# Cross-attention and slot experts on one core: which queue loads the context of batches 4 to 15

## The chip, the core and the metric

The kernel runs on one core of a Trainium2 chip. A core has a matrix engine (TensorE, in profiles PE, with its weight loads as PEld), a vector engine (VectorE, DVE), a scalar engine with activation tables (ScalarE, ACT), a general engine (GpSimd, POOL) and SyncE (SP), which here does nothing but issue DMAs. Each works through its own instructions in order and waits on semaphores for the others. DMAs can be issued by SP, ACT or POOL; all run on the core's 16 DMA engines.

The metric is the time of one execution on the device in microseconds (us), the median of several runs. Before the change it is 1179.04 us over 3 runs (1178.51 to 1179.66).

## What is computed

16 batches of 100 tokens with 256 features attend to a context of 361 rows each, with 16 heads of 16 features; then a layer of 16 soft experts with 64 slots each follows. All is float32.

```python
x = x + xattn(layernorm(x), ctx, ctx, mask, wq, bq, wk, bk, wv, bv, wo, bo)
x = x + ffn(layernorm(x), ...)

# xattn: q = query @ wq + bq; k = ctx @ wk + bk; v = ctx @ wv + bv; 16 heads
#        softmax(q k^T / 4 + (1 - mask) * -1e9) @ v @ wo + bo
# ffn:   x = layernorm(x) * g + b; se = layernorm(slot_embeds) * scale
#        logits = x . se                                   # 100 tokens x 1024 slots
#        dispatch = softmax over tokens; combine = softmax over slots
#        slots = dispatch^T x
#        eout = (gelu(slots Wg + bg) * (slots Wu + bu)) Wd + bd     # 16 experts
#        out = combine @ eout
```

## The kernel before

**Groups and streams.** The batches go in groups of 2, 2, 4, 4 and 4 (`GROUPS`). For each group the attention of its batches runs first, then the softmaxes over tokens and slots, then the 16 experts on the slots of all its batches. Expert weights (512 KB a piece) are streamed from memory once per group through six buffers (`w_all`, `load_weights`, L1209, issued by SP). While the experts of one group run, the attention of the next is worked in between their matmuls.

**The order is a plan.** The program keeps a model of the engines (`Clock`): every piece of work adds an assumed duration to its engine's time. Each piece is a Python generator wrapped in a `Task`; before it goes on, it yields the time from which it may run. The main loop picks the task that is ready, and TensorE's order, and with it that of every other engine, is the order in which tasks are stepped. So an assumed duration or due time changes no computation, but changes the order of instructions. Before the first expert matmul the loop also emits `warm_up` matmuls (L1329), which compute nothing that is used, where it expects TensorE to be idle. Real waits are made by semaphores, whatever the plan assumed.

**Context and keys.** `load_kv(b)` loads the context of batch b into `c_sb`, of which there are two buffers. For b < 4 the rows come as they are, in two DMAs (L199, L202), and TensorE transposes them (L584). For b >= 4 the context comes in 32 x 32 blocks, so that VectorE's block transpose can turn it (L594, L595): twelve DMAs, for each of four blocks of partitions two of 32 partitions x 11 x 32 elements (L210, 352 pieces of 128 bytes, 44 KB) and one of 32 x 2 x 32 (L213, 64 pieces, 8 KB). `load_kv(b + 1)` is called at the start of `key_work(b)`, which makes keys (`k_ps`, L609) and values (`v_ps`, L669) of batch b. `kv_t[b]` is the time from which the plan lets the transposes of batch b run.

**Attention.** For each batch and each of four blocks of four heads: scores for the row maximum (`maxima`, L781, reduced at L786), the maximum folded into the queries (`queries`, L795 and L797), scores again and exponentials (`exponentials`, L806, L814), product with the values (`values`, L829). `out_work(b)` divides by the sums: a shuffle and a reciprocal on VectorE (L709, L710), a product `cxs` on GpSimd (L713), and for every second block the sum of two (L717, VectorE). Then come the output projection `o_ps` (L722), a normalisation (statistics L436, L437; `rstd` on VectorE, L444, then a power on GpSimd, L447), `xn` (L743, VectorE), its transpose `xn_t` (L748) and `xnT` (L754, ScalarE).

**Dispatch and experts.** `lg` (L938) are the logits; the softmax over tokens has its maximum on VectorE (L963), exponentials on ScalarE (L968), and the product `d_ex` by the reciprocal sums on VectorE for group 0 and GpSimd for later ones (L993). `d_t` (L1016) turns it with TensorE (groups 0 to 2), L1008 with VectorE (groups 3 and 4); `sl` (L1028) are the slots. Expert matmuls are `gp` and `up` (L1275) and `dn` (L1235), with the activation on ScalarE (L1286) and the product on VectorE (L1291); `po` (L1157) combines.

**GpSimd's queue before.** In the first 15 us it clears tiles and issues eight DMAs (parameters at L264 to L267, the slot embeddings at L400). From then on it has only the small products named above, and issues nothing.

The lines that the change is about:

Of the kernel before, what the change touches and what calls it, by code (L numbers as in the profile page):

```python
# [43 lines left out]
SB = 352  # L44
# [85 lines left out]
def xattn_ffn_kernel(  # L130
# [27 lines left out]
    nc = tc.nc  # L158
    ctx.enter_context(tc.manual_schedule())
    ck = Clock(4)  # L160
# [17 lines left out]
    def load_x(g):  # L178

        accs[g] = two.tile([N, NG, D], F32, tag="acc", name="acc", bufs=3)  # L180
        step = 2 if g else 1
        for i in range(0, GROUPS[g], step):
            b = starts[g] + i
            nc.sync.dma_start(
                accs[g][:, i : i + step, :], x[b : b + step].rearrange("b n d -> n b d")
            )
            if b == 0:
                load_kv(0)
        x_t[g] = ck.t["PE"] + 7.0 if g else 3.9

    loads, kv_t = {}, {}

    def load_kv(b):

        c_sb = two.tile([P, 3, D], F32, tag="c_sb", name="c_sb")
        if b < 4:
            nc.sync.dma_start(  # L199
                c_sb[:KC, 0:2, :], kv[b, : 2 * KC].rearrange("(c p) d -> p c d", p=KC)  # L200
            )
            nc.sync.dma_start(c_sb[: S2 - 2 * KC, 2, :], kv[b, 2 * KC :])  # L202
        else:
            c_sb = c_sb.rearrange("p c d -> p (c d)").rearrange("p (k s) -> p k s", k=KD)
            blocks = kv[b, :SB].rearrange("(b y) (k a x) -> a y k b x", y=32, a=4, x=32)
            last = kv[b, S2 - 32 :].rearrange("y (k a x) -> a y k x", a=4, x=32)
            for a in range(4):
                rows = c_sb[32 * a : 32 * a + 32]
                for kd in range(KD):
                    nc.sync.dma_start(  # L210
                        rows[:, kd, :SB].rearrange("y (b x) -> y b x", x=32), blocks[a, :, kd]
                    )
                nc.sync.dma_start(rows[:, :, SB:], last[a])  # L213
        loads[b] = c_sb
        kv_t[b] = ck.t["PE"] + 6.0 if b else 5.4

    w_sb = {}

# [113 lines left out]
    def late_loads():  # L332

        nc.vector.tensor_scalar(mrow, mrow, -1.0, 1e9, ALU.add, ALU.mult)
        ck.run("DVE", 0.35)
        nc.sync.dma_start(mrow_d, mrow)
        load_kv(1)
        nc.sync.dma_start(wo_sb, wo.rearrange("(k p) o -> p k o", p=P))
        nc.sync.dma_start(bo_bc, bo.partition_broadcast(P))
# [230 lines left out]
    def key_work(b):  # L570
# [3 lines left out]
        if b + 1 < B and b + 1 not in loads:  # L574
            load_kv(b + 1)
# [942 lines left out]
```

## Time and profile before

| | us |
|---|---|
| median of 3 runs | 1179.04 |
| the profiled execution | 1181.03 |
| its span, first to last instruction | 1179.2 |
| first use of a block-wise context: L594 of batch 4 | 194.9 |
| first issue of L210, by SP | 55.4 |
| last issue of L213, by SP | 658.9 |
| SP's issues of L210, 96, median | 0.464 |
| SP's issues of L213, 48, median | 0.574 |
| POOL's own DMA issues, 8, shortest and longest | 0.52 and 0.96 |

The span is what the trace covers; the execution's own time has some 1.8 us more around it. Times in the profile are counted from the span's start. An engine's busy share is the union of its instructions' times. "Idle before" in a timeline line, in square brackets, is how long the engine had nothing to do before the instruction, with what ended that wait. SP's and ACT's issues of DMAs don't count as busy; on POOL a DMA shows as an instruction that holds the engine. A float32 matmul shows as two passes, so that counts of passes in the trace are twice those of the code for most matmuls.

### The profile page before, as it was taken

The page shows a single profiled execution, that of the slowest core. Times are in us where ns is not written, and L with a number is a line of the kernel's source. Part 1 is how long each engine was busy: PE and PEld are TensorE (multiplying, and loading weights), DVE is VectorE, ACT ScalarE, POOL GpSimd, SP SyncE. Part 2 cuts the span into 40 slices and gives each one's busy share as a digit, 9 for nine tenths or more (in the row PEclk, how much of TensorE's full clock was granted, in tenths as well). Part 3 has the DMA queues.
Part 4 walks back from the last instruction along what each step waited for, and adds up shares of the span by engine and source line. Part 5 has one row for each costly group of instructions (what it writes and reads, how often), then busy time and mean ns, then how long its engine had stood idle before and what let it go on. Part 6 is the DMA issues. An engine that isn't in the chain of part 4 may idle for free.

```text
span 1179.2 us, 24287 instructions
## 1 busy us (share of the span) xinstructions
PE 1160.4 (98%) x9815; PEld 898.6 (76%) x9815; DVE 633.4 (54%) x1559; ACT 540.3 (46%) x1112; POOL 151.4 (13%) x255
## 2 busy tenths in 40 slices
PE   8899999999999999999999999999999999999998
PEld 6588788787788877767777776787878878777876
DVE  5755445566654566655386767656543455432222
ACT  3547553565544667434454634646312336314110
POOL 3110301013000131300010010304000003002000
PEclk9999999999999999999999999999999999999999
DMA  4412666553466603223341321333344343344441
GB/s 133 133 33 83 233 195 202 163 140 120 130 221 224 188 11 90 83 53 106 112 106 54 110 90 39 98 126 112 112 159 138 115 148 126 112 132 159 140 129 55
DMA packets 138578, 144.85 MB, mean 123 GB/s; under 512 B 45040, under 2 KB 97218, under 8 KB 138466
## 3 DMA queue, kind: packets, MB, share of 16 engines
q1 hardware_dynamic: 137358, 141.60, 39.7%
q8 instruction: 78, 1.28, 0.4%
q0 software_dynamic: 496, 1.12, 0.3%
q10 hardware_dynamic: 612, 0.57, 0.2%
q14 instruction: 34, 0.28, 0.1%
HBM read 141.60 MB, written 1.66 MB: 121 GB/s over the span
## 4 chain that ended last, share of the span: by engine, by line
PE 95%; DVE 2%; ACT 2%; issue 1%; DMA 0%; POOL 0%; SPq 0%; ACTq 0%; DVEq 0%; POOLq 0%
PE dn L1235 19%; PE gp L1275 19%; PE up L1275 19%; PE sl L1028 5%; PE po L1157 5%; PE at L806 4%; PE at L781 4%; PE lg L938 3%; PE cx L829 3%; PE k_ps L609 3%; PE v_ps L669 3%; PE o_ps L722 1%; PE at L1329 1%; DVE mxp L786 1%; PE q_ps L538 1%; ACT d_ex L968 1%
## 5 line engine op out<-in xcount | busy, mean ns | idle before, releaser
L1275 PE MATMUL gp<-ring,w_all 128*128 128x256 f32 (+1 forms) x1280 | 247.8, 340 | 1.3 <-ACT lg_all L959 1.3
L1275 PE MATMUL up<-ring,w_all 128*128 128x256 f32 (+1 forms) x1280 | 246.6, 340 | 0.0
L1291 DVE SCALAR_TENSOR_TENSOR hT<-up,parT,ge 128x256 f32<-128x256 f32 (+1 forms) x320 | 119.7, 424 | 233.2 <-PE up L1275 164.3
L1235 PE MATMUL dn<-w_all,hT 128*64 128x256 f32 x2048 | 232.9, 382 | 0.1
L1286 ACT ACTIVATE ge<-gp,parT 128x256 f32<-128x256 f32 (+1 forms) x320 | 117.1, 430 | 249.3 <-PE gp L1275 245.2
L1275 PEld LDWEIGHTS gp<-ring,w_all 128*128 128x128 f32 x1280 | 203.4, 191 | 27.5 <-issue 4.9
L1275 PEld LDWEIGHTS up<-ring,w_all 128*128 128x128 f32 x1280 | 203.7, 191 | 21.4 <-issue 1.2
L1235 PEld LDWEIGHTS dn<-w_all,hT 128*64 128x64 f32 x2048 | 142.7, 137 | 78.5 <-issue 7.8
L786 DVE TENSOR_REDUCE mxp<-at 100x4 f32<-100x1444 f32 x64 | 106.3, 1661 | 30.9 <-PE at L781 30.2
L1244 DVE TENSOR_TENSOR ring<-dn,bd_bc 128x512 f32<-128x512 f32 x64 | 44.3, 692 | 134.8 <-PE dn L1235 133.2
L814 ACT ACTIVATE aT<-at 121x1200 f32<-121x1200 f32 x64 | 75.0, 1171 | 62.9 <-PE at L806 59.5
L1286 ACT ACT_TABLE_LOAD x60 | 77.0, 1283 | 26.7 <-PE gp L1275 26.0
L1008 DVE STREAM_TRANSPOSE disp<-d_ex 32x128 f32<-32x128 f32 x256 | 77.3, 302 | 4.5
L713 POOL TENSOR_TENSOR cxs<-cxs,rs 128x100 f32<-128x100 f32 x63 | 24.9, 398 | 389.3 <-DVE rs L710 361.9
L1043 ACT ACTIVATE ring<-sl,parT 128x256 f32<-128x256 f32 x64 | 32.7, 562 | 67.8 <-PE sl L1028 65.5
L1028 PE MATMUL sl<-disp,xn 100*128 100x256 f32 x256 | 63.4, 388 | 0.2 <-ACT disp L1021 0.2
L1157 PE MATMUL po<-ring,lg_all 128*100 128x256 f32 x256 | 60.5, 383 | 0.4 <-DVE ring L1244 0.2
L993 POOL TENSOR_TENSOR d_ex<-d_ex,d_sm 128x400 f32<-128x400 f32 x28 | 23.9, 854 | 267.6 <-DVE d_sm L990 240.6
L806 PEld LDWEIGHTS at<-q,kT 32*121 32x121 f32 x1344 | 40.6, 180 | 19.9 <-issue 8.8
L1028 PEld LDWEIGHTS sl<-disp,xn 100*128 100x128 f32 x256 | 46.4, 190 | 10.3 <-issue 2.6
L806 PE MATMUL at<-q,kT 32*121 32x100 f32 x1344 | 49.9, 277 | 3.4 <-DVE q L797 3.3
L814 ACT ACT_TABLE_LOAD x36 | 46.2, 1283 | 14.2 <-PE at L806 6.2
(152 smaller groups left out, 1268.8 us busy)
## 6 DMA issues: line engine op xcount, KB each, us to landing
w_all<-in_L_ffn_Wg_dram SPq DMA_DIRECT2D x80, 512.0 KB
w_all<-in_L_ffn_Wu_dram SPq DMA_DIRECT2D x80, 512.0 KB
w_all<-in_L_ffn_Wd_dram SPq DMA_DIRECT2D x80, 512.0 KB
bd_bc<-in_L_ffn_bd_dram SPq DMA_DIRECT2D x80, 64.0 KB
c_sb<-in_ctx_dram SPq DMA_DIRECT2D x96, 44.0 KB
out_dram<-acc SPq DMA_DIRECT2D x8, 200.0 KB
acc<-in_x_dram SPq DMA_DIRECT2D x7, 200.0 KB
ring<-n_L_ffn_slot_embeds_dram POOLq DMA_DIRECT2D x1, 1024.0 KB, 6.8
```

Of the source, the lines that this page charges most:

```text
L781: nc.tensor.matmul(self.at[:N, r, :S2], lhsT=self.q[rows], rhs=self.k[rows], start=True, stop=True)
L786: nc.vector.tensor_reduce(mxv[:, :, m : m + 1], self.at[:N, :, :S2], AX.X, ALU.max, negate=True)
L806: nc.tensor.matmul(self.at[: KC + 1, r, c * N : (c + 1) * N], lhsT=self.k[rows, c * KC : c * KC + KC + 1], rhs=self.q2[rows], start=True, ...
L814: nc.scalar.activation(self.aT[: KC + 1], self.at[: KC + 1, :, : 3 * N], AF.Exp)
L1008: nc.vector.transpose(dst[toks, :, :, a, :], src[32 * a : 32 * a + 32, :, :, toks])
L1028: nc.tensor.matmul(sl[:, kd * 256 : (kd + 1) * 256], lhsT=xns[g][:, b0 + i, kd * P : (kd + 1) * P], rhs=disp[:, i, :], start=True, stop=True,)
L1157: nc.tensor.matmul(pos[i][:N, :D], lhsT=lg_all[:, slot, 2 * c + i, :], rhs=eouts_of(g, q)[:, c, 2 * p + i, :], start=c == 0, stop=c == 1,)
L1235: nc.tensor.matmul(dn[S * x : S * x + S, i * D : (i + 1) * D], lhsT=hts[x][fc // FB][0].rearrange("p (f b s) -> p f b s", f=FB, s=S)[:, fc ...
L1244: nc.vector.tensor_tensor(eouts_of(g, q)[:, j // 2, 2 * half : 2 * half + 2, :], dn.rearrange("p (b d) -> p b d", d=D), biases[k // 2].uns ...
L1275: nc.tensor.matmul(ps[:, f * T : (f + 1) * T], lhsT=w[:, kd, fc * P : (fc + 1) * P], rhs=slots_of(g, q)[:, j, kd].rearrange("p b s -> p (b ...
L1286: nc.scalar.activation(ge[:, cols], ps[:, cols], AF.Gelu, bias=col(8, e, fc))
L1291: nc.vector.scalar_tensor_tensor(out=hT[:, cols], in0=ps[:, cols], scalar=col(NPAR, e, fc), in1=ge[:, cols], op0=ALU.add, op1=ALU.mult,)
```

## The change

The twelve loads of batches 4 to 15 are issued on GpSimd's queue. The plan is told: 12 x 0.6 us are added to GpSimd's time at each of these loads, and their transposes may run 14 us of planned TensorE time after the call, instead of 6.

```diff
             for a in range(4):
                 rows = c_sb[32 * a : 32 * a + 32]
                 for kd in range(KD):
-                    nc.sync.dma_start(
+                    nc.gpsimd.dma_start(
                         rows[:, kd, :SB].rearrange("y (b x) -> y b x", x=32), blocks[a, :, kd]
                     )
-                nc.sync.dma_start(rows[:, :, SB:], last[a])
+                nc.gpsimd.dma_start(rows[:, :, SB:], last[a])
         loads[b] = c_sb
-        kv_t[b] = ck.t["PE"] + 6.0 if b else 5.4
+        if b >= 4:
+            ck.run("POOL", 12 * 0.6)
+        kv_t[b] = ck.t["PE"] + (14.0 if b >= 4 else 6.0) if b else 5.4
```

Because the plan's times differ, the order of instructions differs on every engine from batch 4's load on. The counts are the same but for 144 DMA issues that move from SP to POOL, 6 more of the `warm_up` matmuls (54 for 48), 6 more activation table loads on ScalarE (126 for 120), and one copy of values (L680) that is on VectorE where it was on ScalarE (L683). On GpSimd, the first load's twelve issues stand between two `cxs` products (L713) of batch 1:

```
TensorTensor cxs<-cxs,rs 128x100
DMACopy c_sb<-in_ctx_dram 32x11x32 x2
DMACopy c_sb<-in_ctx_dram 32x2x32
...
TensorTensor cxs<-cxs,rs 128x100
TensorTensor rstd<-rstd,neghalf 100x1
```

## What was predicted

> **What bounds the kernel now.** I read the page's busy line and its chain of work first, then windows by stage, then the waits of PE, then the timeline around the place where the change first acts. Line numbers are those of the kernel before; the changed kernel's are two higher from L217 on.
>
> ```profile
> PE 1160.4 (98%) x9815; PEld 898.6 (76%) x9815; DVE 633.4 (54%) x1559; ACT 540.3 (46%) x1112; POOL 151.4 (13%) x255
> PE 95%; DVE 2%; ACT 2%; issue 1%; DMA 0%; POOL 0%; SPq 0%; ACTq 0%; DVEq 0%; POOLq 0%
> ...
> 0.00:90.00 90.00, 80.52 (x787) 61.28 (x788) 54.21 (x144) 43.43 (x92) 20.59 (x57) 0.98 0.35 101
> 90.00:390.00 300.00, 298.42 (x3186) 239.28 (x3186) 163.47 (x400) 163.98 (x333) 35.59 (x58) 1.00 0.55 173
> 390.00:450.00 60.00, 57.66 (x417) 44.88 (x415) 36.74 (x90) 40.05 (x116) 17.82 (x24) 1.00 0.27 71
> ```
>
> TensorE is busy 98% of the span and is 95% of the chain. The windows (length, then busy time of PE, PEld, DVE, ACT, POOL, then granted clock, DMA share, GB/s) show where the 18.8 us without PE work lie: 9.5 before 90 us, 1.6 in the next 300, 2.3 around 390 to 450 (the same view has 1.0 between 600 and 630 and 4.3 after the last matmuls). The clock is 1.00 after the start, so it takes no part. Two things follow. A transfer that comes sooner can win next to nothing: no DMA ends a wait of PE among PE's waits. And the start is a bare chain: what is late there comes off no slack, because from about 84 us (the first expert matmul) PE has as much work as it can do until the end.
>
> **What leaves SyncE.** 144 issues, 96 of L210 at a median 0.464 us and 48 of L213 at 0.574, together 96 x 0.464 + 48 x 0.574 = 72 us of SP's time. Gain: 0. SP's own waits say why.
>
> ```profile
> SPq L1209 <- PE dn L1235: 349.7, 34, 26.2
> SPq L1209 <- PE gp L1275: 222.3, 42, 13.8
> ```
>
> Issuing the expert weights (L1209), SP waits for TensorE to give weight buffers back; it isn't short of time. Had PE been waiting for weights, up to the 2.3 us of the window 390 to 450 could come back; I take nothing. What stood behind these issues on SP comes sooner, by up to the 6.9 us that the first load took (55.4 to 62.3): the x rows of L184 at 62.3, first read at 73.8, so that wins nothing. The bytes and their 36,864 pieces of 128 B (12 loads of 8 x 352 + 4 x 64) are the same.
>
> **What arrives on GpSimd.** Twelve loads of 12 issues. How long one holds the engine is not in the trace for 352 pieces of 128 B. The rows nearest to it:
>
> ```profile
> 5.76 0.74 POOL L264 DMA_DIRECT2D ring<-in_L_ffn_slot_g_dram  x1
> ...
> 7.05 0.52 POOL L264 DMA_DIRECT2D ring<-in_L_ffn_norm_g_dram  x1
> ...
> 8.67 0.57 POOL L266 DMA_DIRECT2D ring<-in_L_ffn_bu_dram  x1
> 9.21 0.60 POOL L267 DMA_DIRECT2D sc_bc<-in_L_ffn_scale_dram  x1
> ...
> 11.76 0.96 POOL L400 DMA_DIRECT2D ring<-n_L_ffn_slot_embeds_dram  x1
> ```
>
> Second column: us held. Two pieces take 0.52 to 0.74, 64 take 0.57, 128 take 0.60, 1024 take 0.96, and each starts when the one ahead ends: issues on POOL are serial. Between 0.56 and 0.96, 352 pieces stand at 0.56 + 0.40 x 352/1024 = 0.70, and L213's 64 at 0.56. A load is then 8 x 0.70 + 4 x 0.56 = 7.8 us of POOL. Bounds: 12 x 0.52 = 6.2 and 8 x 0.96 + 4 x 0.74 = 10.6. In all some 94 us (75 to 128) on an engine that is 13% busy; as a sum this costs nothing, as a block in an in-order queue it does.
>
> The changed order gives the POOL issues eight completion semaphores in turn, so the ninth issue waits for the first to land. POOL's landings in the trace took 2.0 to 4.7 us, and 6.8 for 1 MB; eight issues take 6 x 0.70 + 2 x 0.56 = 5.3. I take 0 for it, and 6.8 - 5.3 = 1.5 per load at the far end.
>
> POOL's other work shows no disturbance: L713 took 395/397/403 ns (minimum, median, maximum) over 63 executions, with VectorE busy 54% around it. [...]
>
> **Where the first block stands.** load_kv(4) is called when batch 3's keys begin. SP ran ahead and issued it at 55.4. In POOL's new order the 12 issues stand behind the cxs product (L713) of 65.17 and ahead of the next one.
>
> ```profile
> 65.17 0.40 POOL L713 TENSOR_TENSOR cxs<-cxs,rs 128x100 f32<-128x100 f32 x1 [0.53 <-DVE rs L710]
> ...
> 67.39 0.40 POOL L713 TENSOR_TENSOR cxs<-cxs,rs 128x100 f32<-128x100 f32 x1 [1.82 <-DVE rs L710]
> ...
> 69.03 0.25 DVE L717 TENSOR_TENSOR cxs<-cxs 128x100 f32<-128x100 f32 x1
> ...
> 69.53 1.03 PE L722 MATMUL o_ps<-wo_sb,cxs 128*100 128x256 f32 x4
> ...
> 73.92 0.39 PE L748 MATMUL xn_t<-ident,xn 100*128 100x100 f32 x2
> ...
> 75.03 1.18 PE L938 MATMUL lg<-xnT,seT 128*128 128x200 f32 x6
> ```
>
> Step A: the block runs from 65.57 to 65.57 + 7.8 = 73.4; the product to 73.8; the sum L717 to 74.1; the output projection o_ps starts at about 74.3 where it was 69.53: 4.8 us late. Nothing covers it: k_ps and v_ps stand behind o_ps on PE, and the matmuls just ahead of it (L1329) are filler that computes nothing. Also behind the product on POOL are both rstd (L447), which the same chain needs later. At the bounds A is 3.2 and 7.6.
>
> Step B: the new order also puts the last two v_ps matmuls and 6 more fillers ahead of lg, and on DVE two copies of v_ps ahead of xn. From o_ps: 0.86 + 0.45 filler + 1.22 + 1.73 + 0.45 + 0.88 (their parts of the chain of waits) = 5.6, then copy 0.42, xn 0.40 and two hand-overs, xn_t at about 6.7, lg 1.1 later: 7.8. Before, o_ps to lg took 75.03 - 69.53 = 5.5. B = 2.3; at the least 1.0, if the copy doesn't hold xn.
>
> **The other eleven blocks** meet a PE that has expert work, except where a group of batches changes. There the ninth batch's neighbours matter: the new POOL order is rstd, 12 issues, then two d_ex products (L993) that the transposes d_t (L1016) await. PE has between them k_ps 2.8, o_ps 1.0, x_t 0.5, v_ps 2.9, q_ps 1.5 = 8.7 us; the block and one product are 7.8 + 0.85 = 8.7. So 0, and at 10.6 a stall of 2.8; a second such spot follows within the same group: another 2.8. The loads are needed late: the changed plan allows 14 us from call to use, against 7.8 + 4.7 = 12.5. Six more table loads on ACT (126 for 120) at 1283 ns are 7.7 us on an engine idle 54%; were that cover gone they would cost these 7.7.
>
> **Sum.** 4.8 + 2.3 + 0 = 7.1 us on a profiled execution of 1181.03 (span 1179.2 and 1.8 around it): 1188.1. That execution was 2.0 above the median 1179.04, so the median becomes 1186.1. Low end: 3.2 + 1.0 = 4.2, 1183. High end: 7.6 + 2.3 + 2.8 + 2.8 = 15.5, or with 1.5 of landing at three spots instead 11.6: 1194.5.
>
> **Rivals.** *The issue is dearer than any row* (256 more pieces than L267, short ones, eight in a row). At 1.2 and 0.8 a block is 12.8: A 9.8, B 2.3, two stalls of 12.8 + 0.85 - 8.7 = 5.0 each: 22 us, 1201. For it: the price does grow with the pieces. Against: 1024 pieces took 0.96. *Not slower:* the engine is free again long before its issue is done. The product of 67.39 has slack to L717 at 69.03, so A is zero if twelve issues fit in 69.03 - 0.40 - 65.57 = 3.1 us, 0.26 each; then the new order, with 1.6 + 2.3 + 1.0 = 4.9 us of idle PE between 90 and 630 us to win back, ends at 1174 to 1180. Against: the serial rows above, and a MEMSET that follows L400 only after its 0.96. *The load lands after its use*, in the changed plan's 14 us: the transposes (L594) then hold VectorE's queue; if weight traffic delayed the last landing to 16, 2 us at each of twelve loads, 24, and A and B: 31 in all, 1210. Against: SP's first load, among the same traffic, was issued from 55.4 to 62.3 us, and no L594 waited more than 1.1 us for its data. That the loads don't move at all is excluded by the order.
>
> **How the numbers follow.** Forecast 0.58 (1183 to 1194), dearer issue 0.22, late landing 0.07, not slower 0.13. 0.2% is 2.4 us, about what a measurement here tells from no change. Faster by more needs the rival below 1176.7: 0.03; within it the rest of that case: 0.10; slower 0.87. The range takes the forecast, two thirds of the dearer case and the upper edge of no change: 1181.5 to 1199.
>
> **What would show it.** Right: 12 POOL issues behind a cxs of about 65 us, held 0.6 to 0.8 each; o_ps at 74 and the first gp about 7 us later than before; PE busy time the same; later stalls only at d_t. Wrong: issues under 0.3 us or over 1; o_ps on time; a wait of PE for a DMA; L594 waiting for c_sb; or a start as told and an end that gives it back.

## The result, and the profile after

The changed kernel takes 1189.37 us (median of 4 executions, 1188.26 to 1190.71) where the kernel before takes 1179.22 (4 executions, 1178.51 to 1179.66): a ratio of 1.0082, 95% interval 1.0069 to 1.0096. Two further sets of executions gave 1.0070 (1.0056 to 1.0085) and 1.0073 (1.0059 to 1.0086). The profiled execution took 1188.49, with a span of 1186.6: 7.4 more than the span before. Lines from L217 on stand two higher than in the kernel before: `cxs` is L715, its sum L719, `o_ps` L724, `lg` L940, `gp` L1277.

The page's busy line and chain:

```profile
PE 1164.3 (98%) x9827; PEld 901.6 (76%) x9827; DVE 635.3 (54%) x1560; ACT 547.1 (46%) x1117; POOL 239.3 (20%) x399
PE 93%; ACT 3%; DVE 1%; DMA 1%; POOL 1%; issue 1%; SPq 0%; DVEq 0%; ACTq 0%
```

The windows (length, then busy time of PE, PEld, DVE, ACT, POOL, then granted clock, DMA share, GB/s):

```profile
0.00:90.00 90.00, 77.12 (x752) 56.78 (x753) 52.08 (x140) 37.49 (x76) 27.95 (x69) 0.96 0.33 95
90.00:390.00 300.00, 298.24 (x3163) 240.58 (x3163) 164.79 (x402) 162.69 (x337) 64.96 (x106) 1.00 0.53 169
390.00:450.00 60.00, 57.59 (x521) 44.01 (x518) 36.89 (x88) 36.12 (x102) 27.48 (x42) 1.00 0.31 98
```

POOL is busy for 88 us more, the 144 issues. After 90 us TensorE's busy share is what it was (298.24 for 298.42, 57.59 for 57.66), so most of the time is lost ahead of that. There its idle time grew only from 9.5 to 12.9 us; the rest must be time in which TensorE was busy, but slower or with other work. The clock of that window, 0.96 for 0.98, points to the first of these.

The timeline of POOL and of PE around the first block (start, duration, and in brackets the idle time before with what ended it):

```profile
64.22 0.40 POOL L715 TENSOR_TENSOR cxs<-cxs,rs 128x100 f32<-128x100 f32 x1 [0.53 <-DVE rs L712]
65.25 1.36 POOL L210 DMA_DIRECT2D c_sb<-in_ctx_dram  x2 [0.64 <-PE c_t L586]
66.61 0.56 POOL L213 DMA_DIRECT2D c_sb<-in_ctx_dram  x1
...
70.84 1.29 POOL L210 DMA_DIRECT2D c_sb<-in_ctx_dram  x2
72.12 0.56 POOL L213 DMA_DIRECT2D c_sb<-in_ctx_dram  x1
72.70 0.41 POOL L715 TENSOR_TENSOR cxs<-cxs,rs 128x100 f32<-128x100 f32 x1
```

```profile
67.25 1.50 PE L1331 MATMUL at<-ident 128*128 128x128 f32 x12
68.58 0.59 PE L724 MATMUL o_ps<-wo_sb,cxs 128*100 128x256 f32 x2
73.46 0.91 PE L724 MATMUL o_ps<-wo_sb,cxs 128*100 128x256 f32 x2 [4.28 <-DVE cxs L719]
74.16 1.06 PE L1331 MATMUL at<-ident 128*128 128x128 f32 x4
75.02 2.45 PE L611 MATMUL k_ps<-cT,wk 128*128 128x361 f32 x4
...
81.43 1.52 PE L940 MATMUL lg<-xnT,seT 128*128 128x200 f32 x8
...
90.52 1.72 PE L1277 MATMUL gp<-ring,w_all 128*128 128x128 f32 x14
```

The block waits 0.64 us for its buffer, issues for 7.43 us, and the product behind it comes at 72.70 where it came at 67.39. The second half of `o_ps` waits 4.28 us for it. Behind that wait the same matmuls take longer than they did: four fillers 1.06 us for 0.61, `k_ps` 2.45 for 1.38. The windows of that stretch have the granted clock in the same column as above:

```profile
72.00:74.00 2.00, 0.54 (x2) 0.49 (x3) 0.26 (x1) 0.00 (x0) 1.09 (x3) 0.94 0.20 49
74.00:75.00 1.00, 1.00 (x5) 0.91 (x5) 0.56 (x2) 0.00 (x0) 0.00 (x0) 0.50 0.00 0
75.00:76.00 1.00, 1.00 (x4) 0.69 (x3) 0.93 (x4) 0.00 (x0) 0.22 (x1) 0.50 0.00 0
76.00:77.00 1.00, 1.00 (x3) 0.51 (x2) 0.88 (x5) 0.00 (x0) 0.34 (x1) 0.50 0.00 0
77.00:78.00 1.00, 1.00 (x6) 0.75 (x5) 0.49 (x1) 0.00 (x0) 0.94 (x3) 0.91 0.00 0
```

Before, each window between 60 and 90 us had 1.00. The lost clock adds up to 0.06 x 2 + 0.50 x 3 + 0.09 = 1.7 us, which is 3.4 us at a granted clock of 0.50.

**A yardstick for the runs below.** Whole traces are shifted against each other at the start (the first of the two products stands at 65.17 before, at 64.22 here, between 62.4 and 66.5 in all). So the span is cut in three at the start of that product and at the start of the first `gp` matmul, both from the trace (rounded after the subtraction). The last column is the span less the first two.

| run | to cxs | cxs to gp | gp to the end |
|---|---|---|---|
| before | 65.17 | 19.04 | 1095.0 |
| after | 64.22 | 26.30 | 1096.1 |
| a0_after, the same again | 63.69 | 27.60 | 1096.7 |
| a1_after, the same again | 66.54 | 26.32 | 1095.9 |
| e1_plan_only | 64.57 | 20.09 | 1095.3 |
| e2_queue_only | 66.33 | 25.24 | 1112.6 |
| e3_first_on_sync | 64.24 | 19.04 | 1097.6 |
| e4_filler, 18 products | 62.55 | 24.63 | 1096.0 |
| e8_filler_again, 18 | 64.91 | 24.66 | 1096.8 |
| e7_filler9, 9 products | 62.97 | 24.64 | 1097.3 |
| e9_filler9_again, 9 | 62.41 | 26.32 | 1097.2 |
| e5_half_block | 63.26 | 20.96 | 1096.2 |
| e6_block_later | 64.31 | 19.04 | 1096.6 |

In the first profile the change costs 7.26 us between the first product and the first `gp`, and 1.1 behind it. The first column, a stretch that is the same program in all, differs by the clock: its mean from 8 to 62 us is 1.00 in the five traces with 62.4 to 63.7, 0.97 in the six with 64.2 to 65.2 (before and after among them) and 0.94 in the two with 66.3 and 66.5.

### The profile page after: what moved, and what is told of

Its sections match the earlier page's. It is cut to its first block, busy times and chain, and to the rows that moved or that the text cites. A ratio compares the mean times of both kernels' runs of the same rounds, so it can differ in the third digit from the quotient of the medians.

```text
span 1186.6 us, 24343 instructions
## 1 busy us (share of the span) xinstructions
PE 1164.3 (98%) x9827; PEld 901.6 (76%) x9827; DVE 635.3 (54%) x1560; ACT 547.1 (46%) x1117; POOL 239.3 (20%) x399
## 4 chain that ended last, share of the span: by engine, by line
PE 93%; ACT 3%; DVE 1%; DMA 1%; POOL 1%; issue 1%; SPq 0%; DVEq 0%; ACTq 0%
PE dn L1237 19%; PE gp L1277 19%; PE up L1277 18%; PE sl L1030 5%; PE po L1159 5%; PE at L808 4%; PE at L783 4%; PE v_ps L671 3%; PE lg L940 3%; PE k_ps L611 3%; PE cx L831 3%; PE o_ps L724 1%; PE at L1331 1%; ACT d_ex L970 1%; DVE mxp L788 1%; PE q_ps L540 1%
## 5 line engine op out<-in xcount | busy, mean ns | idle before, releaser
L1277 PE MATMUL gp<-ring,w_all 128*128 128x256 f32 (+1 forms) x1280 | 248.0, 341 | 1.3 <-ACT lg_all L961 1.3
L1277 PE MATMUL up<-ring,w_all 128*128 128x256 f32 (+1 forms) x1280 | 246.5, 339 | 0.2 <-DVE c_mx L1079 0.2
L1277 PEld LDWEIGHTS gp<-ring,w_all 128*128 128x128 f32 x1280 | 203.3, 191 | 26.9 <-issue 5.7
L1277 PEld LDWEIGHTS up<-ring,w_all 128*128 128x128 f32 x1280 | 204.3, 191 | 22.1 <-issue 1.7
L715 POOL TENSOR_TENSOR cxs<-cxs,rs 128x100 f32<-128x100 f32 x63 | 24.9, 397 | 325.6 <-DVE rs L712 255.0
L210 POOL DMA_DIRECT2D c_sb<-in_ctx_dram x96 | 62.6, 654 | 2.4 <-issue 0.8
```

Source lines behind the costliest of these rows:

```text
L210: nc.gpsimd.dma_start(rows[:, kd, :SB].rearrange("y (b x) -> y b x", x=32), blocks[a, :, kd])
L1277: nc.tensor.matmul(ps[:, f * T : (f + 1) * T], lhsT=w[:, kd, fc * P : (fc + 1) * P], rhs=slots_of(g, q)[:, j, kd].rearrange("p b s -> p (b ...
```

## The experiments

### The plan or the queue: one part of the change alone

The first run of this set is the changed kernel itself, beside the variants on one chip.

> The changed kernel once more, beside the kernel before and the three variants on one chip. Theory: 1188 to 1191 us, 9 to 11 us over before; first block of twelve DMA issues on GpSimd about 7.4 us, TensorE idle 4.3 us ahead of o_ps, granted clock near 0.5 for about 3 us behind that idle time. If the fall of the clock was an accident of the one profiled execution, it is absent here and the start loses 2 us less.

Measured: 1188.47 us against 1180.51, which is 8.0 over it, where 9 to 11 were expected; the median itself lies in its range. The wait of `o_ps` is 4.3 us again, and the clock falls again, for longer: 0.54 in 72 to 74, 0.50 to 78, 0.75 in 78 to 80, or 3.4 us of full clock lost instead of 1.7. It was no accident of one execution, but its length varies.

The change has two parts, and each was tried without the other. The plan without the queue:

```diff
-                    nc.gpsimd.dma_start(
+                    nc.sync.dma_start(
...
-                nc.gpsimd.dma_start(rows[:, :, SB:], last[a])
+                nc.sync.dma_start(rows[:, :, SB:], last[a])
```

> The changed plan (7.2 us booked on GpSimd and a due time 14 us out for each load from the fifth batch on), but every transfer issued by SyncE as before. Theory (the time is lost to the twelve issues in GpSimd's queue): no wait of TensorE for cxs, no fall of the clock, 1179.5 to 1182 us; what is above 1179 is the price of the altered order alone. Rival (the altered order costs the time): 1186 to 1190 us.

The queue without the plan:

```diff
-        if b >= 4:
-            ck.run("POOL", 12 * 0.6)
-        kv_t[b] = ck.t["PE"] + (14.0 if b >= 4 else 6.0) if b else 5.4
+        kv_t[b] = ck.t["PE"] + 6.0 if b else 5.4
```

> The transfers from the fifth batch on issued by GpSimd, but with the plan of before, which knows nothing of them. Theory (the queue): the first block holds cxs as it did, o_ps waits about 4.3 us, the clock falls, and later blocks may hold work that the plan no longer puts behind them: 1185 to 1195 us. Rival (the plan): 1179 to 1181 us.

Measured: the plan alone 1180.37 us, ratio 1.0005 (0.9994 to 1.0016), no difference that can be told. The order alone costs 20.09 - 19.04 = 1.05 us at the start, by its six more fillers and the tail of `v_ps` ahead of `lg`. The queue alone 1205.26, ratio 1.0213 (1.0198 to 1.0228). So the queue costs the time, as the theory has it; but it had 1195 at most, and its size was missed. The start costs 25.24 - 19.04 = 6.2, as much as it should without the order's part. The other 17.6 us are lost after the first `gp`. The run's waits of PE (in all, times, longest):

```profile
PE v_ps L669 <- DVE kT L630: 4.8, 1, 4.8
PE o_ps L722 <- DVE cxs L717: 4.3, 1, 4.3
PE d_t L1016 <- POOL d_ex L993: 4.1, 2, 3.4
...
PE q_ps L538 <- ACT xT L524: 3.0, 2, 2.3
```

The longest of them, read back through the timelines of POOL, DVE and PE:

```profile
610.90 0.85 POOL L993 TENSOR_TENSOR d_ex<-d_ex,d_sm 128x400 f32<-128x400 f32 x1 [0.39 <-DVE d_sm L990]
611.70 1.32 POOL L210 DMA_DIRECT2D c_sb<-in_ctx_dram  x2
...
618.24 0.56 POOL L213 DMA_DIRECT2D c_sb<-in_ctx_dram  x1 [1.53 <-DMA c_sb<-in_ctx_dram]
...
621.61 0.86 POOL L993 TENSOR_TENSOR d_ex<-d_ex,d_sm 128x400 f32<-128x400 f32 x1
```

```profile
622.51 0.61 DVE L1008 STREAM_TRANSPOSE disp<-d_ex 32x128 f32<-32x128 f32 x2 [6.38 <-POOL d_ex L993]
```

```profile
625.21 1.78 PE L669 MATMUL v_ps<-wv,cT 128*121 128x256 f32 x4 [4.84 <-DVE kT L630]
```

The block stands between two `d_ex` products of POOL, and takes 9.9 us because it also waits twice (1.53 and 0.95 us) for earlier landings. DVE's transpose waits for the second product and holds DVE's queue, where `kT` stands behind it; `v_ps` waits for `kT`. Behind this wait the clock fell once more (0.50 from 625.53 to 632.36, 3.4 us of full clock lost), as it had behind the 3.4 us wait of `d_t` (0.50 from 413.91 to 417.32, 1.7 lost). The changed plan is thus worth 1205.26 - 1188.47 = 16.8 us: it moves the later blocks to where little waits for them. It doesn't do so for the first block. Its two parts, the booked time and the later due time, were left out together, so what each is worth isn't shown.

### Which of the twelve blocks

Only the first moved load back on SyncE, with its plan entry of before (`b > 4` in place of `b >= 4`):

```diff
+            queue = nc.sync if b == 4 else nc.gpsimd
...
-                    nc.gpsimd.dma_start(
+                    queue.dma_start(
...
-        if b >= 4:
+        if b > 4:
```

> The changed kernel with the first of the twelve moved loads (batch 4) back on SyncE with its old plan entry; eleven loads stay on GpSimd. Theory (nearly all the time is lost at the first load): the first gp matmul starts as early as before and the time is 1179 to 1182 us. Rival (each load costs its share): about one twelfth of the loss comes back, 1188 us or more.

Measured: 1182.63 us, ratio 1.0020 (1.0011 to 1.0030), 0.6 above the theory's range and far from the rival's. The start is that of the kernel before to the hundredth, 19.04. Some 2 us stay with the eleven others: from `gp` to the end 1097.6 for 1095.0, of which 1.6 us are waits of `d_t` (L1019) for POOL's `d_ex`, in two places, where the kernel before had 0.6 and the plan alone none.

### The length of the block, and its place

Half of the first block on SyncE, with plan and order as in the changed kernel:

```diff
+                queue = nc.sync if b == 4 and a >= 2 else nc.gpsimd
```

> The changed kernel with six of the twelve issues of the first moved load back on SyncE; plan and order unchanged. Theory (length of the block, 0.62 us an issue, decides): block about 3.8 us, cxs about 3.7 us earlier than in the changed kernel, o_ps waits about 0.6 us, no fall of the clock, 1181.5 to 1184 us. Rival (a block of any length costs much the same): 1186 us or more.

Measured: 1182.46 us, ratio 1.0023 (1.0013 to 1.0033). POOL's timeline:

```profile
64.30 1.36 POOL L211 DMA_DIRECT2D c_sb<-in_ctx_dram  x2 [0.64 <-PE c_t L587]
65.65 0.57 POOL L214 DMA_DIRECT2D c_sb<-in_ctx_dram  x1
66.21 1.29 POOL L211 DMA_DIRECT2D c_sb<-in_ctx_dram  x2
67.49 0.57 POOL L214 DMA_DIRECT2D c_sb<-in_ctx_dram  x1
68.08 0.41 POOL L716 TENSOR_TENSOR cxs<-cxs,rs 128x100 f32<-128x100 f32 x1
```

Six issues take 3.8 us, `o_ps` waits 0.62 us for 4.28, the clock stays at 1.00, and the start costs 1.92 us of the 7.26. Of the 1.92, 1.05 is the order.

All twelve issues on POOL again, but called after the sum `acc<-acc+bo_bc` of batches 2 and 3, and not at the start of batch 3's keys:

```diff
         for i in range(n):
             with_bo[b + i] = t
+        if b == 2:
+            load_kv(4)
...
-        if b + 1 < B and b + 1 not in loads:
+        if b != 3 and b + 1 < B and b + 1 not in loads:
```

> The changed kernel with the first moved load issued later in GpSimd's queue: all twelve issues still on GpSimd, but behind the sum acc<-acc+bo_bc, after which GpSimd had nothing to do for over 35 us. Theory (the place of the block, not its existence, costs the time): no wait of o_ps, start as with the first load on SyncE, 1180.5 to 1184 us. Rival (GpSimd's issues cost the time wherever they stand, through the work behind them): 1186 us or more.

Measured: 1182.01 us, ratio 1.0013 (1.0002 to 1.0023). POOL's timeline:

```profile
64.31 0.40 POOL L717 TENSOR_TENSOR cxs<-cxs,rs 128x100 f32<-128x100 f32 x1 [0.53 <-DVE rs L714]
66.53 0.40 POOL L717 TENSOR_TENSOR cxs<-cxs,rs 128x100 f32<-128x100 f32 x1 [1.82 <-DVE rs L714]
...
77.03 1.27 POOL L565 TENSOR_TENSOR acc<-acc,bo_bc 100x512 f32<-100x512 f32 x1 [1.69 <-DVE z L506]
78.24 1.36 POOL L210 DMA_DIRECT2D c_sb<-in_ctx_dram  x2
```

The same issues, 13 us later, cost the start nothing: 19.04. The later call also books the block later in the plan, and the order of the start is that of before again, so that the 1.05 us of the order are gone too. Place and length decide, and not that POOL issues.

### The clock behind the wait

18 products of the identity with itself, whose results nobody reads, keep TensorE busy through the wait, but for 0.28 us of it:

```diff
+        if b == 1:
+            for _ in range(18):
+                nc.tensor.matmul(at_all[:, 3, 384:], lhsT=ident, rhs=ident, start=True, stop=True)
```

> The changed kernel plus 18 products of the identity with itself, whose results nobody reads, placed ahead of o_ps of batch 1, where TensorE idles for 4.3 us; TensorE stays busy through the wait, and cxs comes no earlier. Theory (a part of the loss is the granted clock, which falls to 0.50 behind the idle time): no window under 0.95 between 66 and 80 us, first gp matmul 2 to 3 us earlier than in the changed kernel, 1185 to 1187 us. Rival (the wait is the whole loss): 1188 to 1190 us, or more by what the added products cost.

The same with `range(9)`:

> As the run with 18 added products, but nine, which leave about 2.2 us of idle time ahead of o_ps. With the plan of before on GpSimd's queue, an idle time of 2.3 us (ahead of q_ps) was followed by a granted clock of 1.00 and one of 3.4 us (ahead of d_t) by 0.50. If the length of the idle time decides: no fall of the clock and the same time as with 18, 1185 to 1187 us. If any idle time of this kind lowers the clock: 1187.5 us or more, windows of 0.50 behind o_ps.

Measured: 1187.36 us with 18 (1184.96 to 1190.12) and 1187.14 with nine (1185.72 to 1189.91), where the changed kernel had 1188.47 (1186.35 to 1189.98) on another chip. The traces are plain: the clock is 1.00 in both, and from cxs to `gp` 24.63 and 24.64 us remain of 26.30 and 27.60. PE's timeline with 18:

```profile
66.91 4.18 PE L724 MATMUL at<-ident 128*128 128x128 f32 x36
...
71.80 0.68 PE L727 MATMUL o_ps<-wo_sb,cxs 128*100 128x256 f32 x2 [0.28 <-DVE cxs L719]
...
72.76 1.38 PE L611 MATMUL k_ps<-cT,wk 128*128 128x361 f32 x4
```

The medians are not plain: 0.1 to 0.4 above the range expected, and the executions overlap. So both were repeated beside the changed kernel.

> The changed kernel again, for more executions beside the two that follow: 1187 to 1190.5 us in the median; from the first cxs to the first gp matmul 26 to 28 us, windows of granted clock 0.50 behind o_ps.

> The 18 added products again. In the trace of the first run they saved 1.7 to 3.0 us between the first cxs and the first gp matmul (24.6 us against 26.3 and 27.6), in the median only 1.1 us with overlapping ranges. If the clock costs what the traces say: 24.6 us again there, and a median 1.5 to 3 us under the changed kernel in this call. Rival (given back later): the median within 1 us of it.

> The nine added products again, by the same two readings: 24.6 us between the first cxs and the first gp matmul, and a median 1.5 to 3 us under the changed kernel, or within 1 us of it if the gain is given back later.

Measured: the changed kernel 1189.58 us, with 18 products 1187.48, with nine 1187.44. Over all three sets of executions the medians are 1189.2 (16), 1187.5 (11) and 1187.3 (12), 1.7 to 1.9 apart, and the means with 18 products 1.4 us lower (standard errors 0.4 and 0.5, so 1.3 us of uncertainty at 95%). The theory's size holds, by a narrow margin; its range there (1.5 to 3 us) was met by 2.1 for both. The granted clock of each execution says the same: the full clock lost, (1 - clock) x span, is 3.4 us in the mean of the 16 executions of the changed kernel, 1.4 with 18 products and 1.8 with nine.

With nine products the second trace showed something else than the first. In both, TensorE idled 2.29 us ahead of `o_ps`; PE's timeline of the first, then of the second:

```profile
72.22 0.68 PE L727 MATMUL o_ps<-wo_sb,cxs 128*100 128x256 f32 x2 [2.29 <-DVE cxs L719]
...
73.18 1.38 PE L611 MATMUL k_ps<-cT,wk 128*128 128x361 f32 x4
```

```profile
71.67 0.93 PE L727 MATMUL o_ps<-wo_sb,cxs 128*100 128x256 f32 x2 [2.29 <-DVE cxs L719]
...
73.24 2.43 PE L611 MATMUL k_ps<-cT,wk 128*128 128x361 f32 x4
```

The same idle time left the clock alone once and halved it once, and cost 26.32 - 24.64 = 1.7 us the second time. So its length alone doesn't decide at 2.3 us, and the expectation that it does falls.

The traces show where the clock changes. In each of the 13 it does so only at times that lie whole steps of 3.4133 us apart, wherever the kernel's work stands: in the run with the queue alone at 75.99, 79.40, 413.91, 417.32, 625.53 and 632.36 us, the later ones 1, 99, 100, 161 and 163 steps behind the first. Windows cut along these steps (columns as above), in the second trace with nine products and then in the first:

```profile
68.54:71.95 3.41, 1.12 (x7) 0.66 (x6) 0.26 (x1) 0.00 (x0) 2.76 (x5) 1.00 0.25 58
71.95:75.36 3.41, 3.41 (x10) 2.51 (x9) 2.37 (x9) 0.00 (x0) 0.64 (x2) 0.50 0.00 0
```

```profile
67.81:71.22 3.41, 2.12 (x18) 1.70 (x16) 0.00 (x0) 0.00 (x0) 3.41 (x6) 1.00 0.27 61
71.22:74.64 3.42, 2.42 (x12) 1.85 (x13) 1.83 (x7) 0.00 (x0) 0.97 (x3) 1.00 0.07 16
```

In the second trace the idle time lies whole in one step, with 1.12 us of work left in it, and the next step is at half clock. In the first it is divided between two steps with 2.12 and 2.42 us of work, and the clock stays. Where the steps fall against the kernel differs from execution to execution: with nine products one ends 0.28 us behind the start of `o_ps` in the second trace (71.95, 71.67) and 1.00 us ahead of it in the first (71.22, 72.22). In a0_after, where the fall lasted twice as long, the step behind the wait (72.18 to 75.59) had 0.74 us without work, and the clock stayed at 0.50 for a second step; that the one made the other wasn't tried. The work in a step alone doesn't tell either: behind one with 1.54 us (499.24 to 502.65 with the queue alone) the clock stayed at 1.00, behind one with 1.59 (5.60 to 9.02 in the kernel before) and one with 2.35 (25.98 to 29.40 in the changed kernel) it was 0.50.

## Why the prediction was right in sign and sum, and where it was not

**Price of an issue.** Put at 0.70 and 0.56 us from POOL's own rows, 7.8 for a block. Measured: L210 625/669/771 ns (minimum, median, maximum) over 96, L213 564/564/644 over 48, 7.43 us for the first block. Right, and with it the rival of a dearer issue falls (1.2 and 0.8 us). So does the one that needed at most 0.26 us.

**VectorE beside the issues.** The prediction took the rows of L713 (395/397/403 ns, with VectorE busy 54%) as a sign that POOL's work isn't disturbed. No issue took over 771 ns, with VectorE busy 54% of the span again, and the mean of L715 is 397 ns for 398 before. Right here for the issues; whether any of the landings, which took up to 7.8 us, were held back by what VectorE did isn't shown, and none of these runs tried vector instructions of other forms.

**Step A, the first block.** Put at 4.8 us. The wait is 4.28; what it moves at the start, with the clock left out, is 24.63 - 20.09 = 4.5 (18 products against the plan alone). Right. It left out the 0.64 us for the buffer, which the cheaper block and the half of `o_ps` that could run ahead of the wait outweighed.

**Step B, the changed order.** Put at 2.3 us. This is the step that failed: the plan alone costs 1.05 there (its `o_ps` to `lg` is 75.57 - 68.92 = 6.65 us, 1.15 over the 5.50 of before, not 7.8), which is the least that I had allowed for it, 1.0, in the case that the copies don't hold `xn`. There the two copies and `xn` run on DVE from 73.04 to 74.13 us, while PE works on `v_ps` until 74.48, so PE never waits for them, where I had put their time behind it. In its place stood a cost that no step had: the clock behind the wait, 1.7 us in two traces of the changed kernel and 3.0 in the third (26.30, 26.32 and 27.60, less 24.6). I had written that the clock takes no part, from windows of a kernel in which TensorE never idled that long once it had started. A + B was 7.1, the sum of the three 4.5 + 1.05 + 1.7 = 7.3: the sum came out by two errors of opposite sign, which was luck.

**The other eleven blocks.** Put at 0, at most two stalls of 2.8 us at `d_t`. Measured from `gp` to the end: 1095.3 us with the changed plan on SyncE, 1095.9 to 1097.6 with the eleven on POOL, so 0.6 to 2.3 us. In the eight traces with the changed kernel's order behind `gp`, this excess over 1095.3 and the wait of `d_t` (0.76 in the first profile, 2.03 at most) agree within 0.5 us. The kind and the place were right, the value between my two; the term that made it is the wait for a landing, below. Much of what I credited to the engines' slack was the plan's doing: without its entries for POOL, and with the order that this gives, 17.6 us are lost behind `gp`.

**Landings.** Expected 2.0 to 4.7 us, with 0 for the wait of a later issue on an earlier landing. Measured for L210 2.1/3.0/7.8, and L213 on POOL waited 5.0 us for them in 4 places. One of these stands in the block ahead of the two `d_ex` products for which I had computed a stall of 0; POOL, then PE, in the first profile:

```profile
404.28 0.56 POOL L213 DMA_DIRECT2D c_sb<-in_ctx_dram  x1 [0.92 <-DMA c_sb<-in_ctx_dram]
...
406.70 1.67 POOL L995 TENSOR_TENSOR d_ex<-d_ex,d_sm 128x400 f32<-128x400 f32 x2
```

```profile
407.62 0.64 PE L1018 MATMUL d_t<-ident,d_ex 128*100 128x128 f32 x4 [0.76 <-POOL d_ex L995]
```

The block's wait for landings and that of `d_t` go together from trace to trace: 0.92 and 0.76 us here, 1.30 and 1.15 with the first load on SyncE, 2.17 and 2.03 in the second trace with nine products, and within 0.2 us in eight of the ten traces with such a block (0.22 and 0.97 with half of the first block on SyncE, 0.28 and none with the first block later). So the 0 was too small; the far end, 1.5 a load, was nearer. No transpose of the changed kernel waited for its data on VectorE, where one did for 1.1 us before, so the rival of a late landing falls. That the rows of SyncE came sooner won nothing, as told.

**The time.** The profiled execution was forecast at 1188.1 and took 1188.49. The median was forecast at 1186.1, 3.3 under the 1189.37 measured (the range was 1181.5 to 1199), because I took 2.0 us off: the profiled execution before stood that much above its median. The changed kernel's stood 0.9 below its own. Much of this spread is the clock's: of the twelve executions of the plan alone, the seven with a granted clock of 0.999 or 1.000 took 1179.3 to 1180.6 us, the five with 0.997 or 0.998 1181.9 to 1184.0. That it is all of it wasn't shown.

**What stays open.** What in a step of 3.4133 us makes the clock fall behind it, why some landings took up to 7.8 us, and what the booked time and the due time of the plan are each worth. No version here beats the kernel before; the plan alone, with the issues on SyncE, is level with it.

## What to carry to other kernels

A DMA issue on GpSimd held that engine's queue here for 0.67 (L210) or 0.56 us (L213) in the median: price such an issue from the engine's own rows, times the number issued together, and look at what stands directly behind the block and who waits for that; here the same twelve issues cost the start some 6 us or nothing, by their place. Where a later issue of the block waited for an earlier landing, that wait was added to the block's length (1.53 and 0.95 of 9.9 us with the queue alone). If the order comes from a plan, book the issues in it, and look at the first block by itself. And when a wait is added to the engine that sets the time, count what its clock does afterwards, not the wait alone (here 1.7 to 3.4 us of full clock lost behind 4.3 us).

## What the runs showed of the hardware that was not expected

Behind 4.3 us of idle time TensorE's granted clock was 0.50, in all three traces of the changed kernel: for 3.4 us in two of them and 6.8 in one (1.7 and 3.4 us of full clock lost, each time from the windows). In the run with the queue alone 3.4 us of idle time did the same, and 2.3 us (ahead of `q_ps`) did nothing; with nine products 2.3 us once did and once didn't. In all 13 traces the clock changed only in steps of 3.4133 us. With nine products it fell in the trace whose idle time lay whole in one step, and stayed in the one where two steps shared it. The step ahead of a fall wasn't always empty: it had 1.12 us of work in the second trace with nine products, and 0.31 and 0.51 in two traces of the changed kernel, ahead of the fall behind the 4.3 us wait.
